# Layer 3's shared products of the first half behind the third quarter's experts, layer 0's later scans with their factor in PSUM, and layer 2's early adds left out

## The chip, the cores and the metric

The kernel runs on one core of one Trainium2 chip. The metric is device time in microseconds (us), the median over runs of the whole program; lower is better. All arithmetic is in float32 on the engines PE (matrix products), DVE (elementwise work on vectors), ACT (activation functions and copies) and POOL; SP only starts plain DMAs. POOL here does little but start indirect DMAs: each of its DMA_INDIRECT instructions scatters or gathers 128 rows of 128 numbers by a list of row positions.

## The reference: four layers over one stream of tokens

The input x has 4 batches of 1024 tokens of width 128. Each of the four layers adds a mixer, normalises, adds a feed-forward part, and normalises again:

```
x = layernorm(x + L0_attn(x)); x = layernorm(x + L0_ffn(x))
x = layernorm(x + L1_attn(x)); x = layernorm(x + L1_ffn(x))
x = layernorm(x + L2_attn(x)); x = layernorm(x + L2_ffn(x))
x = layernorm(x + L3_attn(x)); x = layernorm(x + L3_ffn(x))
```

- L0 mixer: running sums along the tokens. For each of 4 angles, a real and an imaginary part: `cumsum(p_w * poly * cos(phi))` and the same with the sine, both divided by `cumsum(p_w)`, then normalised, projected and gated. That is 8 running sums and one denominator over 1024 tokens.
- L0 feed-forward: one product of 128x128 with quantised operands.
- L1 mixer: a diagonal state-space recurrence. L1 feed-forward: 16 experts of which 4 are chosen for a token, and a shared network.
- L2 mixer: causal attention with 16 heads. L2 feed-forward: 8 experts, 2 chosen, on a common base.
- L3 mixer: products with Toeplitz matrices. L3 feed-forward, the one that the change reorders:

```
sel = expert_out at the 4 chosen of 32 experts;  out = sum(sel * topk_scores)
out = out + silu(flat @ sgate_w.T) * (flat @ sup_w.T) @ sdown_w.T     # shared, hidden width 512
```

## The kernel before: two orders laid over each other

**Tiles and parts.** The tokens are 32 tiles of 128 rows, held in SBUF as `self.x`. A quarter q is 8 tiles (two of each batch, 256 tokens along the sequence). Layer 0 and layer 3 work by quarters or halves: part a is quarters 0 and 1, b is quarter 2, c is quarter 3. Layer 1 has a and the rest r; layer 2 has parts a2, m2, n2.

**How experts are reached.** A router gives each token its experts and a position in a list in device memory. `spread` scatters the rows of a part into that list (one DMA_INDIRECT for each tile and choice, by `indirect`, L1327). The expert stage loads groups of 4 list tiles (`xg`, through SP's queue), multiplies them and writes its results to a second list. `collect` (L1437 and after) gathers for each token tile the rows of its chosen experts into a buffer `yt` and adds them to x on DVE (L1452). Its buffers come from a pool `yp` of 5 or 8.

**When collect adds.** An add is emitted when a landing is expected by the planner's clock `self.now`: while more than one tile is gathered, `self.spacing` is set (the caller wrapped the generator in `spaced`, which also makes each indirect DMA wait for the landing of the one two before it), and the oldest is due, the loop at L1466 adds at once. If all buffers are full it must add the oldest; what is left is added at the end. `spaced` collects occur in layer 1 (`l1_close`) and in layer 2 (`rows_in(a2)` beside `l2_attn(1)`, `rows_in(m2)` beside `l2_experts(n2)`).

**The order of the work.** All engines run their instructions in the order in which the program emits them. `mix(main, side, pace)` emits a main generator and, after each of its steps, lets a side generator advance by an amount given by the two generators' yields and the pace; `queued` fixes the emitted order on every engine. `press` advances the side until something is ready. So the pair (main, side) and the pace decide where on each engine's queue a side step stands.

**Layer 0's second half.** `l0_attn((2, 3))` runs as main with `spread("l1", a)` (64 scatters) beside it. Within it `prepare(q)` makes three products z in PSUM: the value xv (project(0)), the gate (project(1)) and the spread weight pwx; later rsx takes the same pool. Pool "l0z" holds two z buffers of [128 x 1024], two banks of PSUM each. `l0_scan` (L361 to L369) is the running sum: DVE's tensor_tensor_scan of out = keep * previous + source, where `keep` is a [128 x 1024] tile in SBUF, one except for zeros at the first token of each batch. For the denominator `den` the source is z in PSUM; for the real and imaginary parts (`s`) it is a tile in SBUF.

**The end.** In `all` (L2020 and after) the side generator `on` holds, in order: attention, routing and spread of b; then, side by side, `last(a)` (collect of a's 16 tiles, and `finish(a)`, the final normalisation and output, as soon as "shared l3a" is marked) and attention, routing and spread of c; then `last(b)`. The main sequence is experts(a), shared(a), shared(b), experts(b), shared(c), experts(c), close(c). `l3_shared` has 4 blocks of 512 tokens for a and 2 for b and c; a block is 4 rounds of products with `glu` (silu at L763, product `hs` at L764) and a product back (`py`). For a the result is added to x on DVE (L1768); for b and c it is kept in a tile `sh` by ACT (L1771), and `held` adds it when the experts begin. Experts stages end in an If that handles lists longer than expected; it holds work for all engines and is a border for the order of emission.

Of the kernel before, what the change touches and what calls it, by code (L numbers as in the profile page):

```python
# [15 lines left out]
ALU = mybir.AluOpType  # L16
AX = mybir.AxisListType
PSUM = bass.MemoryType.PSUM
DRAM = bass.MemoryType.DRAM

P = 128
# [10 lines left out]
QC = QT * P  # L32
# [3 lines left out]
KH, HC, MF, CK = 32, 4, 4, 4  # L36
# [38 lines left out]
class Kernel:  # L75
# [282 lines left out]
        for b in range(B):  # L358
            self.mm(ps[32 * b : 32 * b + 32, :], w, src[:, b * TQ : (b + 1) * TQ], start, stop)

    def l0_scan(self, out, src, i, q):  # L361

        nc = self.nc
        first = lambda a: a.rearrange("p (b t) -> p b t", b=B)[:, :, 0]
        if q:
            nc.vector.tensor_tensor(first(src), first(src), self.sums[:, i, :], ALU.add)
        nc.vector.tensor_tensor_scan(out, self.keep.rearrange("p b t -> p (b t)"), src, 0.0, ALU.mult, ALU.add)
        if q + 1 < NQT:
            nc.scalar.copy(self.sums[:, i, :], out.rearrange("p (b t) -> p b t", b=B)[:, :, TQ - 1])  # L369

# [7 lines left out]
    def l0_attn(self, qs):  # L378

        nc, tc, col = self.nc, self.tc, self.col
        ts, tt = nc.vector.tensor_scalar, nc.vector.tensor_tensor
        x, x0T, taps, cb = self.x, self.x0T, self.taps, self.col["conv_b"]
        with ExitStack() as ctx:
            bp, tp, psy = self.l0_bp, self.l0_tp, self.l0_psy
            psz = self.pool(ctx, "l0z", 2, space=PSUM)
            pss = self.side

            def prepare(q):  # L390
                z2 = self.tile(pss, [P, BLK], "s")[:, :TQ]
                for k in range(CK):
                    for b in range(B):
                        self.mm(
                            z2[32 * b : 32 * b + 32, :], taps[:, k, 2 * P :], x0T[:, q, b, k : k + TQ],
                            k == 0, k == CK - 1,
                        )
                pw = self.tile(bp, [P, TQ], "pw")
                ts(pw, z2, cb[:, 2:3], col["score"], ALU.add, ALU.mult)
                ts(pw, pw, -20.0, 20.0, ALU.max, ALU.min)  # L400
                nc.scalar.activation(pw, pw, AF.Exp)
                tt(pw, pw, self.tw[:, q, :], ALU.mult)

                def project(ch):
                    z = self.tile(psz, [P, QC], "z")
                    for h in range(2):
                        for k in range(CK):
                            self.mm(
                                z[:, h * BLK : (h + 1) * BLK].rearrange("p (b t) -> p b t", b=2),
                                taps[:, k, ch * P : (ch + 1) * P],  # L410
                                x0T[:, q, 2 * h : 2 * h + 2, k : k + TQ],
                                k == 0,
                                k == CK - 1,
                            )
                    return z

                z = project(0)
                xv = self.tile(bp, [P, QC], "xv")
                nc.scalar.activation(xv, z, AF.Identity, bias=cb[:, 0:1])
                z = project(1)  # L420
                gate = self.tile(bp, [P, QC], "gate")
                nc.scalar.activation(gate, z, AF.Silu, bias=cb[:, 1:2])
                pwx = self.l0_spread(psz, pw)

                pq = self.tile(bp, [P, QC], "pq")
                ts(pq, xv, self.nw2, self.dw[:, 1:2], ALU.mult, ALU.add)
                tt(pq, pq, xv, ALU.mult)
                nc.vector.scalar_tensor_tensor(pq, pq, self.dw[:, 0:1], pwx, ALU.add, ALU.mult)
                den = self.tile(bp, [P, QC], "den", bufs=1)
                self.l0_scan(den, pwx, 2 * MF, q)  # L430
                ts(den, den, 1e-4, None, ALU.max)
                nc.scalar.activation(den, den, AF.Square)
                return xv, gate, den, pq

            made = self.l0_made
            if not made:
                made[qs[0]] = prepare(qs[0])
                yield (20.0,)
            for q in qs:
                xv, gate, den, pq = made.pop(q)  # L440
                ms = self.tile(pss, [P, BLK], "s")[:, :TQ]
                self.l0_by_head(ms, self.headd, den, True, False)
                yv = self.tile(psy, [P, QC], "yv")
                for m in range(MF):

                    k = self.tile(tp, [P, QC], "k")
                    nc.scalar.activation(k, xv, AF.Identity, scale=self.turn[:, m : m + 1], bias=self.rnd)
                    nc.scalar.activation(k, k, AF.Identity, bias=self.drop)
                    nc.vector.scalar_tensor_tensor(k, xv, self.turn[:, m : m + 1], k, ALU.mult, ALU.subtract)
                    im = self.tile(tp, [P, QC], "im")  # L450
                    nc.scalar.activation(im, k, AF.Sin, scale=2.0 * PI_IN)
                    nc.scalar.activation(k, k, AF.Abs)
                    re = self.tile(tp, [P, QC], "re")
                    nc.scalar.activation(re, k, AF.Sin, scale=-2.0 * PI_IN, bias=self.halfpi)
                    for part, v in ((1, im), (0, re)):
                        tt(v, v, pq, ALU.mult)
                        s = self.tile(tp, [P, QC], "s", bufs=3)
                        self.l0_scan(s, v, 2 * m + part, q)
                        sq = self.tile(tp, [P, QC], "sq")
                        nc.scalar.activation(sq, s, AF.Square)  # L460
                        first, last = m == 0 and part == 1, m == MF - 1 and part == 0
                        for h in range(2):
                            c = slice(h * BLK, (h + 1) * BLK)
                            self.mm(yv[:, c], self.wbd[:, part * MF + m, :], s[:, c], first, last)
                        self.l0_by_head(ms, self.head, sq, False, last)
                        yield (5.0,)
                    if m == 0 and q + 1 in qs:
                        made[q + 1] = prepare(q + 1)
                        yield (10.0,)
                if q == 1:  # L470
                    self.l0_weight()
                    made[q + 1] = prepare(q + 1)
                rs = self.tile(bp, [P, TQ], "rs")
                nc.scalar.activation(rs, ms, AF.Sqrt, scale=1.0 / (2.0 * HC * MF))
                nc.vector.reciprocal(rs, rs)
                rsx = self.l0_spread(psz, rs)
                for g in range(2):
                    c = slice(g * BLK, (g + 1) * BLK)
                    tt(gate[:, c], rsx[:, c], gate[:, c], ALU.mult)
                    tt(gate[:, c], yv[:, c], gate[:, c], ALU.mult)  # L480
                for g in range(2):
                    po = self.tile(pss, [P, 4, D], "s")
                    for k in range(4):
                        t = g * 4 + k
                        self.mm(po[:, k, :], gate[:, t * P : (t + 1) * P], self.w_out)
                    t0 = q * QT + g * 4
                    tt(x[:, t0 : t0 + 4, :], po, x[:, t0 : t0 + 4, :], ALU.add)
                self.norm(self.quarter(q), by="act", on_act=True)
                yield (10.0,)
# [951 lines left out]
    def collect(self, lay, part, k, yp, first=0, nt=None, which=None):  # L1441

        nc = self.nc
# [3 lines left out]
        late = []  # L1447
# [9 lines left out]
        for t in which or range(first, first + (nt or part.nt)):  # L1457
            yt = self.tile(yp, [P, k, D], "yt")
            for i in range(k):
                self.indirect(  # L1460
                    out=yt[:, i, :], out_offset=None, in_=ys,
# [1 line left out]
                )  # L1463

            late.append((t, yt, self.moved_by + 4.0))
            while self.spacing and len(late) > 1 and late[0][2] <= self.now:  # L1466
                add()
            if len(late) == yp.bufs:
                while late[0][2] > self.now:
# [495 lines left out]
    def all(self):  # L1965
        a, rest = self.first, self.rest
        b, c = rest
        r = self.both[1]
        a2, m2, n2 = self.by_rows
        with ExitStack() as ctx:  # L1970
# [37 lines left out]
            with ExitStack() as c3:  # L2008
# [26 lines left out]
                    self.when(listed("made l3b")), self.last(b, yp),  # L2035
                )
                self.run(self.mix(self.l3_experts(a, wall3), on, 0.45, False))
                self.run(self.mix(self.chain(self.l3_shared(a, sw), self.mark("shared l3a")), on, 0.45, False))
                hold = self.pool(c3, "l3hold", 2)
                for p in (b, c):  # L2040
                    self.press(on, listed("mixed l3" + p.name))
# [3 lines left out]
                    self.press(on, listed("mixed l3c"))  # L2045
                    ahead = self.chain(self.held(p, sh), on) if p is c else self.held(p, sh)
                    self.run(self.mix(self.l3_experts(p, wall3, ahead), on, 0.75, False))
                self.run(self.close(c, yp))
        bad = self.nc.values_load(self.flag[0:1, 0:1], min_val=0, max_val=1)  # L2049
        with self.tc.If(bad > 0):  # L2050
# [181 lines left out]
```

## Time and profile before

| what | value |
|---|---|
| median of 9 runs | 2248.76 us (2236.59 to 2267.42) |
| the profiled execution's own time | 2228.34 us |
| its span | 2226.5 us |
| mean clock granted to PE | 0.849 |
| POOL's DMA_INDIRECT, layer 1's spread of a | 64, from 264.9 to 363.8 us |
| attention and routing of c done, spread of c | 32, from 1936.7 us |
| PE on shared(a), shared(b) | from 1863 to 2014 us |
| PE on experts(b), shared(c), experts(c) | 2017 to 2071, 2072 to 2094, 2097 to 2165 us |
| gathers of the last quarter (close) | 32, from 2170.6 to 2212.4 us |

The profiled execution is 0.9% faster than the median of the runs. A group line of the profile has the source line, the engine, the operation, out<-in by the program's names, and how often it ran, then busy time and the mean time of one in ns, then the idle time of the engine just before these instructions and what ended most of it. A line of the timeline has the start, the time taken, the engine, source line and operation; in brackets stands the idle time of the engine before it and what ended it. "issue" means that the engine waited for nothing that the profile shows; "remote" that what released it couldn't be named.

### The profile page before, as it was taken

The numbers are of one execution on the slowest core, as the hardware profiler recorded it, in microseconds if no ns is written. First come the engines' busy times: TensorE is split into PE (matmuls) and PEld (weight loads), VectorE is DVE, ScalarE is ACT, GpSimd is POOL, SyncE is SP. The second block draws the span as 40 slices with busy tenths as digits, with TensorE's granted clock in tenths as the row PEclk, the third lists the DMA queues.
The fourth block names the chain that finished last, engine by engine and source line by source line (L and its number), as shares of the span: only waits on it lengthen the run. The fifth ranks groups of instructions, "written<-read, shape, count | busy, mean of one in ns | idle before, by whom it ended". The sixth has DMA issues, their size and how long they took to land. (4 is left out here: it accounts for less than half of the span.)

```text
span 2226.5 us, 27104 instructions
## 1 busy us (share of the span) xinstructions
PE 1606.2 (72%) x9025; PEld 951.4 (43%) x9025; DVE 1196.7 (54%) x3491; ACT 903.8 (41%) x1352; POOL 681.6 (31%) x670
## 2 busy tenths in 40 slices
PE   7875864968486387789888788976987956718860
PEld 3332432844232146646522323322655734406650
DVE  8998783656665164436645555463423744503454
ACT  6873551423142263223257565653222631303340
POOL 1000284144406400534250000232463054362225
PEclk9986887988788698889999988997988978868985
DMA  9960012432401105323310000003422321013232
GB/s 296 287 185 1 8 47 91 119 117 98 146 30 50 42 16 195 117 68 88 116 41 8 1 1 1 20 21 146 186 81 82 93 79 53 22 47 105 86 115 58
DMA packets 215530, 187.10 MB, mean 84 GB/s; under 512 B 16528, under 2 KB 194064, under 8 KB 214864
## 3 DMA queue, kind: packets, MB, share of 16 engines
q1 hardware_dynamic: 194672, 142.29, 20.5%
q0 software_dynamic: 20704, 42.86, 5.9%
q8 instruction: 84, 1.38, 0.3%
q14 instruction: 70, 0.57, 0.1%
HBM read 88.49 MB, written 96.60 MB: 83 GB/s over the span
## 5 line engine op out<-in xcount | busy, mean ns | idle before, releaser
L1081 ACT ACTIVATE pr<-sc 128x1024 f32<-128x1024 f32 x288 | 279.7, 1021 | 255.5 <-PE sc L161 178.5
L161 PE MATMUL sc<-qm,kT 32*128 32x512 f32 (+3 forms) x1536 | 212.9, 575 | 44.1 <-ACT pr L1081 40.8
L161 PE MATMUL gu<-ld,xgT 128*128 x640 | 181.6, 431 | 68.3 <-ACT xgT L171 37.9
L161 PE MATMUL s<-pr,va 128*32 128x512 f32 (+3 forms) x1536 | 170.8, 541 | 39.4 <-DVE va L971 16.2
L1087 DVE TENSOR_TENSOR pr<-pr,ld 128x512 f32<-128x512 f32 (+1 forms) x160 | 91.7, 581 | 155.9 <-ACT pr L1081 134.2
L161 PEld LDWEIGHTS gu<-ld,xgT 128*128 128x128 f32 x640 | 129.5, 214 | 98.2 <-ACT xgT L171 49.3
L1814 DVE TENSOR_TENSOR hg<-sg,gu 128x256 f32<-128x256 f32 x160 | 66.3, 416 | 175.0 <-ACT sg L1813 108.7
L161 PEld LDWEIGHTS sc<-qm,kT 32*128 32x128 f32 x1536 | 87.5, 201 | 151.9 <-issue 70.4
L161 PE MATMUL gu<-wall,xgT 128*128 x304 | 148.0, 611 | 3.1 <-issue 1.7
L173 DVE COPY hT<-tp 128x512 f32<-128x512 f32 x118 | 81.0, 687 | 83.9 <-PE tp L169 63.6
L1813 ACT ACTIVATE sg<-gu 128x256 f32<-128x256 f32 x160 | 61.4, 385 | 146.1 <-PE gu L161 78.6
L169 PE MATMUL tp<-ld,hg 128*128 128x128 f32 x624 | 101.3, 283 | 10.8 <-DVE hT L173 7.5
L171 ACT COPY xgT<-tp 128x512 f32<-128x512 f32 x99 | 58.1, 587 | 125.2 <-PE tp L169 69.8
L169 PEld LDWEIGHTS tp<-ld,hg 128*128 128x128 f32 x624 | 80.6, 146 | 60.5 <-issue 36.9
L1569 ACT ACTIVATE sg<-gu 128x512 f32<-128x512 f32 x76 | 45.4, 597 | 145.8 <-PE gu L161 119.4
L161 PEld LDWEIGHTS s<-pr,va 128*32 128x32 f32 x1536 | 37.6, 114 | 145.5 <-issue 81.0
L161 PE MATMUL pu<-xT,ld 128*128 128x512 f32 x104 | 61.1, 678 | 51.8 <-DVE hs L764 51.2
L1327 POOL DMA_INDIRECT l1ra<-x,posl1a x64 | 79.7, 1245 | 60.3 <-DVE peq L1321 41.1
L764 DVE TENSOR_TENSOR hs<-sg,pu 128x512 f32<-128x512 f32 x48 | 32.6, 684 | 116.0 <-remote 70.2
L1327 POOL DMA_INDIRECT l1rr<-x,posl1r x64 | 63.6, 994 | 95.2 <-DVE posl1r L1302 71.3
L1327 POOL DMA_INDIRECT l2rm<-x,posl2m x16 | 15.9, 995 | 250.5 <-DVE peq L1320 243.2
L1571 DVE TENSOR_TENSOR hg<-sg,gu 128x512 f32<-128x512 f32 x76 | 51.9, 683 | 74.8 <-ACT sg L1569 64.1
(446 smaller groups left out, 3526.5 us busy)
## 6 DMA issues: line engine op xcount, KB each, us to landing
wall<-wall SPq DMA_DIRECT2D x16, 768.0 KB
l3ra<-zero SPq DMA_DIRECT2D x1, 6144.0 KB
ld<-in_l_w SPq DMA_DIRECT2D x2, 3072.0 KB
wall<-we SPq DMA_DIRECT2D x24, 256.0 KB
ld<-in_l_w SPq DMA_DIRECT2D x1, 6144.0 KB
l1ra<-zero SPq DMA_DIRECT2D x1, 5120.0 KB
l1rr<-zero SPq DMA_DIRECT2D x1, 5120.0 KB
xg<-l3ra SPq DMA_DIRECT2D x20, 256.0 KB
```

The costliest lines, as they stand in the source:

```text
L161: return self.nc.tensor.matmul(out, lhsT, rhs, start=start, stop=stop)
L169: nc.tensor.transpose(pt[:, k * P : (k + 1) * P], s, self.ident)
L171: nc.scalar.copy(dst, pt[:, : n * P])
L173: nc.vector.tensor_copy(dst, pt[:, : n * P])
L764: nc.vector.tensor_tensor(dst, sg, pu, ALU.mult)
L1081: nc.scalar.activation(pr, sc[h], AF.Exp)
L1087: nc.vector.tensor_tensor(d, d, cst["tril"].unsqueeze(1).unsqueeze(1).to_broadcast([P, 2, n, P]), ALU.mult)
L1327: ins = self.nc.gpsimd.indirect_dma_start(**kw)
L1569: nc.scalar.activation(sg, gu[:, 0, :], AF.Silu)
L1571: nc.vector.tensor_tensor(h, sg, gu[:, 1, :], ALU.mult)
L1813: nc.scalar.activation(sg, pg[:, :, 0, :], AF.Silu)
L1814: nc.vector.tensor_tensor(h[:, 2 * c : 2 * c + 2, :], sg, pg[:, :, 1, :], ALU.mult)
```

## The change

Three edits. First, in the second call of `l0_attn` the pool of z has one buffer instead of two, and the two banks hold `kept`, a copy of `keep` made by ACT; the scans of the real and imaginary parts of quarter 3, and the last three of quarter 2, take their factor from `kept`. The `den` scans and the others keep the SBUF tile. Second, the loop of early adds in `collect` runs for layer 1 only. Third, shared(a) is taken out from between experts(a) and shared(b) and put after experts(b), with pace 0.75 instead of 0.45, and the mark "shared l3a" goes with it.

```
-    def l0_scan(self, out, src, i, q):
+    def l0_scan(self, out, src, i, q, keep):
...
-        nc.vector.tensor_tensor_scan(out, self.keep.rearrange("p b t -> p (b t)"), src, 0.0, ALU.mult, ALU.add)
+        nc.vector.tensor_tensor_scan(out, keep, src, 0.0, ALU.mult, ALU.add)
...
-            psz = self.pool(ctx, "l0z", 2, space=PSUM)
+            psz = self.pool(ctx, "l0z", 1 if qs[0] else 2, space=PSUM)
             pss = self.side
+            held = self.keep.rearrange("p b t -> p (b t)")
+            if qs[0]:
+                keep = self.tile(self.pool(ctx, "l0k", 1, space=PSUM), [P, QC], "kept")
+                nc.scalar.copy(keep, self.keep.rearrange("p b t -> p (b t)"))
+            else:
+                keep = held
...
-                self.l0_scan(den, pwx, 2 * MF, q)
+                self.l0_scan(den, pwx, 2 * MF, q, held)
...
-                        self.l0_scan(s, v, 2 * m + part, q)
+                        self.l0_scan(s, v, 2 * m + part, q, keep if q > 2 or 2 * m + 1 - part > 4 else held)
...
-            while self.spacing and len(late) > 1 and late[0][2] <= self.now:
+            while self.spacing and lay == "l1" and len(late) > 1 and late[0][2] <= self.now:
                 add()
...
                 self.run(self.mix(self.l3_experts(a, wall3), on, 0.45, False))
-                self.run(self.mix(self.chain(self.l3_shared(a, sw), self.mark("shared l3a")), on, 0.45, False))
                 hold = self.pool(c3, "l3hold", 2)
                 for p in (b, c):
                     self.press(on, listed("mixed l3" + p.name))
                     sh = self.tile(hold, [P, QT, D], "sh")
                     self.run(self.mix(self.l3_shared(p, sw, sh), on, 0.75, False))
                     self.press(on, listed("l3" + p.name))
                     self.press(on, listed("mixed l3c"))
                     ahead = self.chain(self.held(p, sh), on) if p is c else self.held(p, sh)
                     self.run(self.mix(self.l3_experts(p, wall3, ahead), on, 0.75, False))
+                    if p is b:
+                        self.run(self.mix(self.chain(self.l3_shared(a, sw), self.mark("shared l3a")), on, 0.75, False))
                 self.run(self.close(c, yp))
```

## The prediction

> **What bounds the kernel now.** I read the engine totals first: no engine is busy all the way, so a stage has to be read by what it waits for.
>
> ```profile
> span 2226.5 us, 27104 instructions
> PE 1606.2 (72%) x9025; PEld 951.4 (43%) x9025; DVE 1196.7 (54%) x3491; ACT 903.8 (41%) x1352; POOL 681.6 (31%) x670
> L1327 POOL DMA_INDIRECT l1ra<-x,posl1a x64 | 79.7, 1245 | 60.3 <-DVE peq L1321 41.1
> ```
>
> The last line is the scatter of the first half's rows into layer 1's expert list: 64 instructions at a mean of 1245 ns, where other groups of the same kind have 978 to 995. The timeline at this group shows why, and what follows it.
>
> ```profile
> 279.55 2.28 DVE L367 TENSOR_TENSOR_SCAN den<-keep,z 128x1024 f32<-128x1024 f32 x1
> 280.77 0.96 POOL L1327 DMA_INDIRECT l1ra<-x,posl1a  x1 [0.30 <-issue]
> ...
> 285.20 2.23 DVE L367 TENSOR_TENSOR_SCAN s<-keep,im 128x1024 f32<-128x1024 f32 x1
> ...
> 285.42 2.78 POOL L1327 DMA_INDIRECT l1ra<-x,posl1a  x1 [0.31 <-issue]
> ...
> 294.43 2.94 POOL L1327 DMA_INDIRECT l1ra<-x,posl1a  x1 [0.30 <-issue]
> ...
> 362.80 0.96 POOL L1327 DMA_INDIRECT l1ra<-x,posl1a  x1 [0.30 <-issue]
> 368.88 0.69 DVE L848 TENSOR_TENSOR x<-py,x 128x512 f32<-128x512 f32 x1 [23.48 <-remote]
> 368.97 0.60 ACT L763 ACTIVATE sg<-pg 128x512 f32<-128x512 f32 x1 [15.37 <-remote]
> ```
>
> A DMA issue beside the `den` scan, whose source z is in PSUM, takes 0.96 us. Beside a scan with both operands in SBUF it takes 2.78 us and ends 0.77 us after the scan. And DVE and ACT, idle for 23.48 and 15.37 us, go on only 5 to 6 us after the scatter's last issue (362.80 + 0.96).
>
> Those waits are on PE's semaphore though PE's matmuls were long over. I looked for the same elsewhere: it happens only in long dense runs of indirect DMAs, most of all near the end. Busy time by window (PE, PEld, DVE, ACT, POOL, then clock, DMA share, GB/s), and the timelines of POOL, PE and DVE around it:
>
> ```profile
> 1900.00:1950.00 50.00, 45.88 (x192) 28.00 (x193) 30.84 (x111) 18.03 (x30) 13.05 (x14) 0.90 0.05 18
> 1950.00:2000.00 50.00, 6.20 (x32) 3.77 (x30) 1.07 (x5) 0.60 (x1) 36.21 (x38) 0.61 0.15 51
> ```
>
> ```profile
> 1936.68 0.99 POOL L1327 DMA_INDIRECT l3rc<-x,posl3c  x1 [33.29 <-ACT sg L763]
> ...
> 1996.54 0.94 POOL L1327 DMA_INDIRECT yt<-l3ya,posl3a  x1 [0.30 <-issue]
> ```
>
> ```profile
> 2004.45 2.07 PE L161 MATMUL pu<-xT,ld 128*128 128x512 f32 x2 [47.92 <-DVE hs L764]
> ```
>
> ```profile
> 2003.70 0.69 DVE L764 TENSOR_TENSOR hs<-sg,pu 128x512 f32<-128x512 f32 x1 [52.63 <-remote]
> ```
>
> While POOL issues 48 indirect DMAs back to back (32 of the spread of quarter c, 16 gathers of part a), PE idles 47.92 us, DVE 52.63. Last, layer 2's second attention call, DVE:
>
> ```profile
> 1122.08 0.35 DVE L1452 SCALAR_TENSOR_TENSOR x<-yt,wkl2a,x 128x128 f32<-128x128 f32 x1 [7.51 <-DMA yt<-l2ya,posl2a]
> 1123.61 0.35 DVE L1452 SCALAR_TENSOR_TENSOR x<-yt,wkl2a,x 128x128 f32<-128x128 f32 x1 [0.84 <-DMA yt<-l2ya,posl2a]
> ...
> 1129.23 0.35 DVE L1452 SCALAR_TENSOR_TENSOR x<-yt,wkl2a,x 128x128 f32<-128x128 f32 x1 [1.32 <-DMA yt<-l2ya,posl2a]
> ```
>
> DVE stands in front of gathered tiles that haven't landed; attention's L1087 multiply is queued behind, and PE waits 6.40 us for that (until 1130.30).
>
> **Part A: scan factor in PSUM.** The 11 scans changed (layer 0, quarter 2's last three and quarter 3's eight) are those whose starts lie between 265.2 and 317.7, inside the scatter (264.9 to 363.8). The 11 issues held by them take 15.8 us more than 0.96 each (1.01, 1.23, 2.57, 1.82, 0.87, 1.98, 1.86, 1.14, 0.91, 1.21, 1.22). With one SBUF operand they should run as beside `den`. Some of that returns: the issues then meet DVE's products with two SBUF operands (L456, 1.22 us; one beside it took 1.81). Stepping the queue at 1.26 us an issue along DVE's rows, the scatter ends 12.5 us sooner. The scan itself costs the same (`den` 2.28, s 2.23 to 2.29). Bounds of the gain: 0 to 15.8.
>
> The Trainium skill, "SBUF — State Buffer", section "Who interferes with whom", says that a VectorE instruction with two SBUF inputs contends with a GpSimd one that reads SBUF and that one with a single SBUF input does not, which agrees; its section "A bandwidth-pool intuition that's wrong (but worth ruling out)" lets the blocked side go on about 115 ns after VectorE's end, where the rows above show 0.77 us. By that figure the 11 issues would lose only about 8.6 us (15.8 less 11 x 0.65), an estimate from that page, and part A would be worth 6 rather than 12.5.
>
> Cost: z has one PSUM buffer, so project(1) (about 6.9 us of PE, 249.2 to 256.1) waits for the copy xv, 249.20 to 250.31: +1.1 us, and behind it on PE stands the router's mask product at 256.24, which leads to the scatter. The later uses have slack: the `den` scan has read z by 281.83, and rsx's matmul starts at 285.34. The copy into `kept` is one ACT pass of 128x1024, 1.04 us by the row of k at 278.43; ACT idles 3.05 us before 239.85, so nothing; uncovered it costs 1.04.
>
> What passes on: 12.5 - 1.1 = 11.4 if the 368.88 release follows the scatter's end. But a denser POOL may bring late PE semaphores into layer 0 itself, which has some 70 us left at 265. Before, with issues each 1.55 us on average, none is late before 339; the replayed pace is 1.32 until 282 and 1.48 until 316. Some lateness there I put at 2: **A = -9**. Bounds: -14.7 (15.8 - 1.1), and on the bad side the lock described as rival 1, +26.
>
> **Part B: layer 2's early adds.** The spaced collects of a2 (32 gathers, 1101.3 to 1159.8) and m2 now add only with all 8 buffers full, after 16 gathers, 25 us in, or at the end. The 12.5 us in which DVE stood on landings (7.51 + 0.84 + 0.86 + 1.26 + 0.76 + 1.32) go; on PE that is 6.40. Next late: the same adds, 16 at 0.35 = 5.6 us, in a bunch ahead of layer 3's attention of a, whose spread starts only at 1476. For m2 (8 tiles) the adds near 1661 to 1681 had no such waits: 0, within 3 either way. **B = -5**; bounds -12.5 and +5.6 (+3 more if m2's bunch shows).
>
> **Part C: shared(a) behind experts(b).** Nothing is added: 4 blocks of some 11 us of PE move. It moves past SP's loads of quarter b's 12 groups of list tiles, which now start earlier (b's scatter is done by 1838.5, so they wait for nothing), and past POOL's queue: first 32 gathers of a, spread c (32), the rest of a's gathers (32), then b's. Working the yields against both paces, c's spread starts in experts(b)'s sixth group, and of a's gathers only 4 follow it at once; the other 12 of the 16 come one tile at a time. The dense run shrinks from 48 to some 36 issues, 45.5 us instead of 60.9. PE's idle time began 19.9 us after the run's start and ended 6.9 after its end, so 47.9 becomes 32.5: -15.4. The run of 32 at 1797.7 to 1838.5 cost PE 24.74, which bounds the gain at 23; 0 if 12 gathers before it join up to 48 again, and below nothing, 10, if POOL's late gathers hold an expert group. The first 32 gathers (1863.4 to 1903.4, 20.75 us of PE idle) stay 32 in a row, now beside shared(b). I take half: **C = -8**. Cover: spread c must land before experts(c); it has about 80 us now and is later by some 50. finish(a) waits for the mark "shared l3a", which now comes after experts(b); by the yields it still falls into experts(c)'s groups 4 to 5, as before, and b's gathers into 6 to 12.
>
> **Sum.** -9 - 5 - 8 = -22 on the profiled execution's 2228.3 (span 2226.5, 1.8 around it), 2206. That execution lies 20.4 us, 0.9%, under the median 2248.8 of nine, so on the median's scale 2248.8 - 22 = **2227**.
>
> **Rivals.**
> 1. Layer 0 locks (slower). Scans no longer hold POOL back, so issues run at 1.26 us and late PE semaphores begin before 300, as in the other dense runs. Then layer 0's last 35 to 45 us run only after the scatter's end near 347, and the step now at 368.88 comes at about 392: +23 instead of -9. With B and C: 2248.8 + 23 - 13 = 2259, up to 2275 without them. For it: runs at 1.29 and 1.26 (1797.7, 1863.4) lock PE within 16 to 21 us. Against it: products and the 1.32 to 1.48 pace remain until 316. It decides from the point where PE's updates stay late for over 13 us before 320.
> 2. The tail (slower): a's finish slips past experts(c)'s sixth group, and b's 32 gathers (1.27 each, 41 us) come in front of the last quarter's 32. 2249 + 41 - 14 = 2276. Against: the computed place is unchanged.
> 3. Absorbed (no change): DVE has 48.5 of 50 us busy at 250 to 300 and sets layer 0's end itself; the dense run re-forms. A, B, C near 0, 2240 to 2255.
> 4. The change doesn't do what it says: a scan from PSUM still holds POOL since its output is in SBUF. A = +1, rest -13: 2237. The `den` row speaks against it.
>
> **Chances.** 2227 case 0.45 (own range 2208 to 2238), rival 1 0.22, rival 2 0.10, rival 3 0.15, rival 4 0.08. About 0.5% (11 us) is what a measurement can tell from nothing. Slower: 0.10 + most of 0.22 = 0.30. Same: rival 3 and part of 1 and 4, 0.17. Faster: the rest, 0.53. The range reaches to 2270: above it most of rival 2 and the extreme of rival 1, 0.12; below 2208, where all gains come near their bounds, 0.06.
>
> **What would show it.** A: issues beside the 11 scans at 0.96 us, scatter's group mean near 1050 ns, its end near 352, the x<-py release near 357 to 360. If its mean falls but the release is later than 369, rival 1. B: no DVE waits on yt near 1115 to 1130, PE's 6.40 gone. C: the longest PE idle near c's spread under 40 us. If it is still 48, or if gathers of l3yb stand among those of l3yc, C is wrong.

## The result: slower by 1.6%, and the profile after

The changed kernel takes 2281.56 us in the median of 20 runs (2254.04 to 2313.18), the kernel before 2248.53 in 62 (2217.11 to 2273.50). The ratio is 1.0159, with a 95% interval of 1.0131 to 1.0187. It was forecast as 2227 and lies outside the range up to 2270. The profiled execution took 2314.1, 1.4% more than its median, so stages are compared in it and not its total.

The group line of the scatter of the first half's rows and busy time by window in layer 0's last quarter (PE, PEld, DVE, ACT, POOL, clock, DMA share, GB/s), of the changed kernel, and below them the middle window of the kernel before:

```profile
L1333 POOL DMA_INDIRECT l1ra<-x,posl1a x64 | 62.7, 980 | 62.2 <-DVE peq L1326 43.0 <-issue 18.6 <-DMA l1ra<-x,posl1a 0.3
```

```profile
250.00:300.00 50.00, 25.76 (x137) 10.49 (x136) 33.56 (x119) 20.39 (x22) 26.23 (x26) 0.78 0.09 33
300.00:350.00 50.00, 1.08 (x8) 0.20 (x8) 0.00 (x0) 3.29 (x3) 36.50 (x38) 0.50 0.13 51
350.00:400.00 50.00, 31.30 (x142) 15.27 (x143) 39.09 (x53) 28.54 (x34) 0.00 (x0) 0.80 0.03 9
```

```profile
300.00:350.00 50.00, 36.45 (x149) 17.09 (x149) 28.41 (x59) 23.38 (x31) 39.49 (x35) 0.84 0.31 116
```

The mean issue fell from 1245 to 980 ns. Part of that is only that DVE does little beside it: from 300 to 350 DVE does nothing, and PE 1.08 us of work (36.45 before). Where DVE works on, the mean is 1068 (E10, below). The product of PE that makes z, DVE's timeline, with what it does on either side of the idle time, and POOL's last issue:

```profile
276.83 1.89 PE L161 MATMUL z<-pw,ld 128*128 128x256 f32 x8
```

```profile
293.17 1.28 DVE L434 SCALAR_TENSOR_TENSOR pq<-pq,dw,z 128x1024 f32<-128x1024 f32 x1 [14.09 <-remote]
...
299.08 0.68 DVE L437 TENSOR_SCALAR den<-den 128x1024 f32<-128x1024 f32 x1
355.20 1.75 DVE L481 RECIPROCAL rs<-rs 128x256 f32<-128x256 f32 x1 [55.44 <-ACT rs L480]
```

```profile
347.10 0.96 POOL L1333 DMA_INDIRECT l1ra<-x,posl1a  x1 [0.30 <-issue]
```

PE has ended z at 278.72. DVE needs it for the first instruction of its lines, but begins that only at 293.17, after 14.09 us of idle time. The profile can't name what released it ("remote"); that it is PE's semaphore is read from what the instruction takes in. The scatter ends 16 us earlier than before (348.1 against 363.8), and layer 0 stands still until 7 us after its end. Layer 1's first x<-py then comes at 407.5 instead of 368.9. The end of the changed kernel, PE's timeline (the three longest idle stretches from 1945 us on):

```profile
1981.29 2.07 PE L161 MATMUL pu<-xT,ld 128*128 128x512 f32 x2 [30.19 <-DVE hs L770]
...
2041.05 3.78 PE L161 MATMUL gu<-ld,xgT 128*128 x8 [17.41 <-issue]
...
2081.73 3.78 PE L161 MATMUL gu<-ld,xgT 128*128 x8 [34.43 <-DVE hT L173]
```

Before, the stretches at the same work were 20.75 and 47.92. Now they are 30.19, and 17.41 + 34.43.

### The profile page after: what moved, and what is told of

Its sections match the earlier page's. It is cut to its first block, busy times and chain, and to the rows that moved or that the text cites. A ratio compares the mean times of both kernels' runs of the same rounds, so it can differ in the third digit from the quotient of the medians.

```text
span 2312.2 us, 27088 instructions
## 1 busy us (share of the span) xinstructions
PE 1600.0 (69%) x9025; PEld 951.4 (41%) x9025; DVE 1197.4 (52%) x3491; ACT 900.9 (39%) x1351; POOL 662.0 (29%) x670
## 5 line engine op out<-in xcount | busy, mean ns | idle before, releaser
L173 DVE COPY hT<-tp 128x512 f32<-128x512 f32 x118 | 81.0, 687 | 87.5 <-PE tp L169 53.6
L1333 POOL DMA_INDIRECT l3ra<-x,posl3a x64 | 64.1, 1002 | 94.0 <-ACT pr L1087 64.2
L161 PE MATMUL yp<-ld,hT 128*128 x640 | 87.0, 278 | 3.5 <-DVE hT L173 3.4
L1333 POOL DMA_INDIRECT yt<-l3ya,posl3a x64 | 61.0, 954 | 97.8 <-DVE x L1458 55.7
L169 PE MATMUL tp<-ld,xg 128*128 128x128 f32 x396 | 69.0, 303 | 26.6 <-DMA xg<-l2rn 5.4
```

The source lines that it names most:

```text
L161: return self.nc.tensor.matmul(out, lhsT, rhs, start=start, stop=stop)
L169: nc.tensor.transpose(pt[:, k * P : (k + 1) * P], s, self.ident)
L173: nc.vector.tensor_copy(dst, pt[:, : n * P])
L1333: ins = self.nc.gpsimd.indirect_dma_start(**kw)
```

## The experiments

Each comparison below is with runs of the kernel before on the same chip, in the same session. The sessions fall into two kinds. In four the median of the kernel before was 2235 to 2273 us, as in the result; in three it was 1932 to 1933. I call the first kind sessions with late handoffs: there PE's semaphore reaches DVE and ACT several microseconds late within POOL's runs of indirect DMAs (it was read so in the prediction, and above for z), in the second kind it doesn't. The number of the chip doesn't tell them apart: chip 9 was met in both.

**Which edit costs: the three alone, and the first without its point.** The first edit alone (E1) has the one z buffer, `kept`, and the 11 scans from PSUM; E2 has only the condition `lay == "l1"`; E3 only moves shared(a). E4 is E1 with

```
-                        self.l0_scan(s, v, 2 * m + part, q, keep if q > 2 or 2 * m + 1 - part > 4 else held)
+                        self.l0_scan(s, v, 2 * m + part, q, held)
```

so that the z buffer and the copy stay and every scan reads its factor from SBUF.

> Before with the first edit alone (one z buffer, the kept copy, 11 scans with the factor in PSUM). Theory 'lock' (POOL's scatter, no longer held up by the scans, runs at 1.26 us an issue and PE's semaphore reaches DVE and ACT late for the rest of the run): the scatter ends near 348, DVE idles over 40 us before it, and the time is 30 to 38 us over before, nearly all that the whole change costs (33). Rival 'end' (most of the loss comes from the shared products moved behind experts(b)): within 12 us of before.

> Before with the second edit alone (early adds for layer 1 only). The profile of the changed kernel shows layer 2's second attention call about 8 us shorter between its gathers of a2 and the spread of m2, then 10 us lost by the spread of n2. Theory: the waits on landings go, the time is 0 to 8 us under before. Rival: the bunched adds come back later and it is 0 to 5 us over before.

> Before with the third edit alone (shared(a) behind experts(b)). Theory 'same density': POOL has the same number of back-to-back indirect DMAs, only beside other work, and PE's idle time moves (47.9 in one piece becomes two pieces of about 17 and 34, the 20.8 before it about 30): 0 to 13 us over before. Rival, as predicted: 8 us under before. Rival 'end': 25 to 33 us over.

> The first edit with its one z buffer and its copy into PSUM, but with every scan's factor read from SBUF as in before. Theory 'lock': the scans hold POOL up again, so the time is that of before plus 0 to 2 us (the single z buffer), the scatter ends near 364. Rival 'z buffer' (what costs is the second product waiting for the first one's copy): 30 us or more over before, as with the whole edit.

Measured, in one session with late handoffs: E1 1.0130 (1.0063 to 1.0197), E2 1.0017 (0.9985 to 1.0048), E3 1.0028 (0.9986 to 1.0069), E4 1.0026 (0.9967 to 1.0085). The three edits add up to 1.75%, the whole change has 1.59%. So the first edit carries the loss, and in it the scans' factor: E4 keeps all the rest and is back at before. The intervals of E1 and E4 overlap by a little, but their traces stand clearly apart: the first x<-py of layer 1 comes at 394.83 in E1 and at 367.20 in E4. "End" and "z buffer" fall. The window 300 to 350 of E1 and then of E4:

```profile
300.00:350.00 50.00, 6.71 (x25) 4.61 (x26) 14.49 (x15) 13.32 (x14) 38.41 (x39) 0.53 0.13 51
```

```profile
300.00:350.00 50.00, 33.89 (x136) 15.40 (x136) 28.92 (x60) 23.83 (x30) 39.34 (x36) 0.82 0.31 116
```

POOL issues hardly more in this window (39 against 36), but over the whole scatter at a mean of 1.33 us instead of 1.52. DVE's idle time between the scatter's first and last issue is 50.7 us in E1, 33.7 in E4, 36.3 in before, 63.5 in the whole change. E1's 394.83 is 26 us after before's 368.88.

In E2 DVE's waits for gathered tiles of a2 fall from 12.6 us to 4.5 (their group by tile, of E2), and the time doesn't move clear of noise:

```profile
L1452 DVE SCALAR_TENSOR_TENSOR x<-yt,wkl2a,x x32: 335/347/365, 1125.3 to 1181.1; 128x128 f32<-128x128 f32 x32
...
  DMA yt<-l2ya,posl2a: 4.5, 4
```

The stage from these gathers to the scatter of m2 is 6.6 us shorter in E2's trace than in before's, but from that scatter to the next one of a it takes 11.8 us more. POOL, on its side, waits 13.8 us for gather buffers where it waited 5.4. What takes the gain back was not followed.

In E3, POOL's timeline at c's scatter shows why the long run did not shrink:

```profile
1936.95 0.95 POOL L1327 DMA_INDIRECT yt<-l3ya,posl3a  x1 [37.02 <-DVE x L1452]
...
1951.10 0.95 POOL L1327 DMA_INDIRECT yt<-l3ya,posl3a  x1 [0.30 <-issue]
1952.36 0.99 POOL L1327 DMA_INDIRECT l3rc<-x,posl3c  x1 [0.30 <-issue]
...
1992.30 0.96 POOL L1327 DMA_INDIRECT l3rc<-x,posl3c  x1 [0.30 <-issue]
1993.57 0.98 POOL L1327 DMA_INDIRECT yt<-l3ya,posl3a  x1 [0.30 <-issue]
```

Twelve gathers before the 32 scatters and four behind are again 48 in a row; PE's idle time there is 22.91 + 29.12 instead of 47.92, and 30.13 instead of 20.75 in the first run.

**Breaking the run by waits.** In `all`, layer 1's scatter of a is wrapped so that every fourth issue waits for the landing of the one before it: E5 on top of the first edit, E6 on before. E7 does it on before to layer 3's scatters of b and c and the gathers of a, E8 to all of these and to the scatter of r (where before already had a wait at every issue, for the landing two before it).

```
-                    self.run(self.mix(self.l0_attn((2, 3)), self.spread("l1", a, K1)))
+                    self.run(self.mix(self.l0_attn((2, 3)), self.spaced(self.spread("l1", a, K1), 4, 1, 1.6)))
```

> The first edit, with layer 1's scatter of part a made to pause: every fourth indirect DMA waits for the landing of the one before it. Theory 'lock by density' (what costs is the unbroken run of issues 1.26 us apart, not the factor in PSUM nor anything else of the edit): with the pauses PE's semaphore arrives in time again, DVE's idle time before the scatter's end goes from about 50 us to under 15, and the time is back at before, within 8 us. Rival 'a queue that is longer by count' (64 DMAs of software descriptors in flight hold PE's semaphore, however spaced): still 25 us or more over before.

> Before, its scans untouched, with the same pauses in that scatter. Theory 'lock by density': the pauses also break the dense second half (from 321 us on), so the 19 to 23 us in which PE, ACT and DVE wait for 368.9 shrink, if the scatter doesn't end later than about 372: 0 to 12 us under before. Rival: the scatter only ends later, 5 to 15 us over before.

> Before, with the same pauses in layer 3's dense runs: the spreads of b and c and the gathers of a (runs of 32, 32 and 48 at 1.26 to 1.29 us an issue, with 24.7, 20.8 and 47.9 us of PE idle). Theory 'lock by density': the three idle stretches fall together by 40 us or more and the time by 20 to 50. Rival 'longer by count': the idle stretches grow with the runs' length, 5 to 30 us over before.

> Before, with the pauses in layer 1's scatters of a and of r and in layer 3's runs. Theory: the gains of the single places add up, and the 37 us of PE idle in the scatter of r (719 to 761) shrink as well: 30 to 70 us under before. Rival: 10 us or more over before.

These met a session without late handoffs: before took 1933.17. E5 0.9960 (0.9944 to 0.9975), E6 1.0017 (1.0003 to 1.0031), E7 1.0082 (1.0065 to 1.0099), E8 1.0107 (1.0090 to 1.0124). So nothing was decided on the lock; what they show is that where layer 3 has no long idle stretches to win back, the pauses cost some 16 us (E7). In E7's trace 56 gathers of b and c stand in one row at the end (1864.8 to 1939.6), most of b's behind experts(c), which PE ends at 1872.5.

**The change itself in such a session.** The same kernels again, with the whole change (E9), the first edit alone (E10), E5's and E7's kernels (E11, E12).

> The whole changed kernel again. The last four runs met a chip on which the kernel before takes 1933 and no handoff of PE is late in any run of indirect DMAs; the ones before it a chip where it takes 2235 and they are. Theory 'lock of the chip' (the loss exists only where PE's semaphore is held up): on a chip of the first sort the changed kernel is 5 to 20 us under before, on one of the second 25 to 40 over. Rival 'order' (the loss is in the order of the work itself): over before by 25 or more on both.

> The first edit alone again. Theory 'lock of the chip': where before takes about 1933, the scatter ends near 348 and layer 1 goes on at once, 7 to 13 us under before; where it takes about 2235, 25 to 35 over. Rival 'order': 25 or more over before on both.

> The first edit with the pauses in the scatter, again. Where before takes 1933 it was 8 us under before. Where before takes 2235: theory 'lock by density': the pauses lift the lock and it is within 10 us of before; rival 'longer by count': 25 us or more over.

> Before with pauses in layer 3's runs, again. Where before takes 1933 there was no PE idle time to win, and it was 16 us over, because a's gathers took POOL longer and b's came after experts(c). Where before takes 2235: theory 'lock by density': the idle stretches of 24.7, 20.8 and 47.9 us shrink by 40 or more together and the time falls by 10 to 40; rival: 10 to 30 us over before.

Before took 1931.69. E9 0.9963 (0.9950 to 0.9977), E10 0.9973 (0.9960 to 0.9985), E11 0.9973 (0.9962 to 0.9984), E12 1.0102 (1.0088 to 1.0117). The same instructions are 0.4% faster than before here and 1.6% slower there: the rival "order" falls, since it asked for the loss in both. The window of E10, to be held beside E1's, which is the same kernel, and its handoff of z:

```profile
300.00:350.00 50.00, 45.39 (x211) 23.67 (x210) 36.76 (x80) 27.69 (x42) 38.78 (x37) 0.91 0.32 120
```

```profile
276.09 1.89 PE L161 MATMUL z<-pw,ld 128*128 128x256 f32 x8
```

```profile
278.30 1.27 DVE L434 SCALAR_TENSOR_TENSOR pq<-pq,dw,z 128x1024 f32<-128x1024 f32 x1
```

POOL issues nearly as densely (1.37 us in the mean over the scatter, 1.33 in E1; its first ten issues 1.29 here and 1.31 there and in the changed kernel), and PE works 45.39 us instead of 6.71. DVE takes z 0.32 us after PE's end, in the changed kernel's profile 14.45 us after it. To the scatter the first edit does what the prediction said: the 64 issues take from 266.3 to 353.8, 87.5 us, against 98.8 for the same scatter of unchanged code in E7, 11.3 sooner where 12.5 were replayed. But the release does not follow the scatter's end here: the first x<-py comes at 339.07, and at 338.70 in E7. What comes sooner are the first results of layer 1's experts, at 380.7 instead of 388.9. Of this 5.2 us are left in the time, where 7 to 13 were expected.

**Waits again.** E13 to E15 are E5's, E7's and E6's kernels, sent to meet the other kind of session.

> The first edit with pauses in the scatter. On a chip with late handoffs (before about 2235): theory 'lock by density' within 10 us of before, DVE idle before the scatter's end under 15 us; rival 'the factor in PSUM' 25 us or more over before, as without pauses. On a chip without: 5 to 8 us under before, as twice already.

> Before with pauses in layer 3's runs. With late handoffs: theory 'lock by density' 10 to 40 us under before; rival 10 to 30 over. Without: 16 to 20 us over, as twice already.

> Before with pauses in layer 1's scatter of a. With late handoffs: theory 0 to 12 us under before. Without: 2 to 4 us over, as once already.

They met one without late handoffs once more (before 1931.77) and repeat: 0.9962 (0.9947 to 0.9976), 1.0092 (1.0063 to 1.0121), 1.0012 (0.9996 to 1.0029).

> The first edit with pauses in the scatter, once more. With late handoffs (before about 2235): theory 'lock by density' within 10 us of before, DVE idle before the scatter's end under 15 us; rival 'the factor in PSUM' 25 us or more over before. Without: 5 to 9 us under before, as three times already.

E16, E5's kernel, met late handoffs (before 2237.62): 1.0116 (1.0037 to 1.0195). By the expectation as written the rival "factor in PSUM" wins. But POOL's timeline shows that the waits did not hold it:

```profile
302.92 0.96 POOL L1333 DMA_INDIRECT l1ra<-x,posl1a  x1 [0.30 <-issue]
304.18 0.96 POOL L1333 DMA_INDIRECT l1ra<-x,posl1a  x1 [0.30 <-issue]
305.44 0.96 POOL L1333 DMA_INDIRECT l1ra<-x,posl1a  x1 [0.30 <-issue]
306.71 0.96 POOL L1333 DMA_INDIRECT l1ra<-x,posl1a  x1 [0.30 <-issue]
```

The issues are still 1.26 us apart; the mean over the scatter is 1.34, as in E1, and DVE is idle for 51.3 us of it, as in E1. Of POOL's idle time in the scatter only 0.3 us ended with a landing. The run was another E1, on another chip, and did not test density. E5 and E11 are no test of pauses either: there the waits moved the mean pace from E10's 1.37 us to 1.40.

**Breaking the run by work.** E17 has the first edit and puts six memsets of a 128x128 tile on POOL after every fifth indirect DMA, ordered behind it and ahead of the next, in layer 1's scatters, layer 3's scatters of b and c and the gathers of a. E18 adds the scatters of a2, m2 and of layer 3's a, and the gathers of b.

```
+    def breathe(self, on):
+        self.rests += on
+        if on and self.rests % 5 == 0:
+            for _ in range(6):
+                m = self.nc.gpsimd.memset(self.pad, 0.0)
...
+                self.moved.append(m.ins.name)
...
+                self.breathe(lay + part.name in ("l1a", "l1r", "l3b", "l3c"))
...
+                self.breathe(lay + part.name == "l3a")
```

> The first edit, and after every fifth indirect DMA of layer 1's scatters (a and r), layer 3's scatters (b and c) and the gathers of a, six memsets of 128x128 on POOL (about 0.23 us each by before's row, so some 1.4 us of rest in 7.7). Waits on landings had not thinned the scatter, this must. With late handoffs (before about 2235): theory 'density' DVE is idle less than 25 us within the scatter of a (the first edit alone: about 50 before its end), layer 1 goes on at most 10 us later than in before, and the idle stretches of r, b, c and a shrink by a third or more; time 0 to 60 us under before. Rival 'the factor in PSUM' or 'count': DVE idle as in the first edit alone, 25 to 60 us over before. Without late handoffs (before about 1932): 5 to 20 us over before, for POOL's longer chains.

> The run before with rests also in the scatters of a2, m2 and of layer 3's a, and in the gathers of b. With late handoffs (before 2235 to 2275): theory 'density': PE's idle stretch near b's gathers (24.5 us) goes below 12 and the time is 6 to 9% under before; rival: it stays, 5 to 6.5% under. Without late handoffs (before about 1932): 5 to 20 us over before, POOL's chains being some 12% longer with nothing to win.

Both met late handoffs. E17: 0.9339 (0.9259 to 0.9419), 2122.49 against 2273.30. E18: 0.8985 (0.8932 to 0.9038), 2031.43 against 2268.26. POOL's timeline and the window of E17:

```profile
304.97 1.36 POOL L1335 DMA_INDIRECT l1ra<-x,posl1a  x1 [0.30 <-issue]
306.64 0.96 POOL L1335 DMA_INDIRECT l1ra<-x,posl1a  x1 [0.30 <-issue]
307.59 1.54 POOL L1385 MEMSET pad<- 128x128 f32 x6
309.29 0.96 POOL L1335 DMA_INDIRECT l1ra<-x,posl1a  x1 [0.16 <-issue]
```

```profile
300.00:350.00 50.00, 44.87 (x203) 23.52 (x204) 37.66 (x81) 27.45 (x41) 39.07 (x69) 0.90 0.30 111
```

The factor is in PSUM as in E1, the 64 scatters are all there, and PE has 44.87 us of work in the window instead of 6.71. What differs are the memsets and the pace that they make, 1.62 us in the mean. So the factor in PSUM is not what holds PE, and neither is the count: it is the unbroken run of issues. Two quite different things break it, POOL's stalls behind the scans (E4) and these memsets (E17); a pause of a third kind was not tried. The scatter ends at 370.4, 18 us later than in E1, and the first x<-py is at 342.1 instead of 394.8, where sessions without late handoffs have it at 338 to 342. (DVE's idle time within the scatter is 32.9, over the 25 that were expected: some 20 of it lie at the end, where DVE waits for a product of POOL's, `qt`, that stands behind the scatter in POOL's queue.) The gain is far over the 0 to 60 us that were expected of E17, and a little over the 6 to 9% of E18. At layer 3's end, where PE did 6.20 us of work in 50 before, it does 41.23 (E18, from c's scatter at 1814.6):

```profile
1815.00:1865.00 50.00, 41.23 (x240) 34.56 (x238) 18.03 (x45) 16.90 (x38) 38.98 (x74) 0.93 0.42 132
```

PE's idle stretches of over 8 us, without the one at the program's start, add up to 193.8 us in before's trace, 307.9 in the changed kernel's, 248.7 in E1, 80.8 in E17 and 67.7 in E18, and in the session without late handoffs to 48.6 in E9 and 38.1 in E10; the one of 24.5 us near b's gathers in E17 is gone in E18. E18 beats the kernel before by 10% in a session with late handoffs (the changed kernel wasn't run there). That is 237 of the 336 us that lie between the 2268 us of the kernel before there and its 1932 us without late handoffs; what the other 100 are was not followed. E18 was not tried in a session without late handoffs, nor was a kernel with these rests and without the first edit, so how much of the 10% the first edit gives or takes is open.

## Why the prediction was wrong

**Part A, the failed step.** The prediction costed late semaphores within layer 0 at 2 us ("Some lateness there I put at 2"), because none was late there before 339 at a mean pace of 1.55, and the replayed pace of 1.32 to 1.48 seemed slow enough until 316. It was not slow enough. In the changed kernel z is late 13 us after the scatter's start (ended by PE at 278.72, taken by DVE at 293.17), and up to there POOL issued 1.31 us apart: the replayed pace of 1.32 came true, what was concluded from it did not. The 1.55 is also a mean over the whole scatter; in its first 26 us the kernel before issues 1.91 us apart. The prediction had named the sign itself, a lower mean issue with a release later than 369, and both came (980 ns, 407.5). That was rival 1, given 0.22: it put the release at 392 and the time at 2259, up to 2275 without B and C. E1 measured 394.8 for the release and +29 us (1.3%), where the rival had +23 for the edit. The choice between the ends failed, not the ends: -14.7 to +26 were on the page, and E1 lies 3 us over the upper one. It was taken from the row of the irregular run, 1.55, where the rows of the dense ones, 1.26 to 1.29, were nearer to the replayed start, 1.32, and these showed PE locked within 16 to 21 us.

The mechanism that the gain was worked from holds for the scatter. In E10 ten issues take over 1.1 us: the very first, and nine that end 0.83 us after a product of DVE with two SBUF operands; none ends so after a scan from `kept`. The scatter is 11.3 us shorter (87.5 in E10, 98.8 in E7); the 82.0 of the change and the 84.7 of E1 count DVE's standstill too. That the release follows the scatter's end holds only where handoffs are late. The Trainium skill, "SBUF — State Buffer", section "Who interferes with whom", agrees in kind: a scan with one SBUF operand no longer delays the DMA issue. The estimate of 6 us made with that page's figure of about 115 ns (section "A bandwidth-pool intuition that's wrong (but worth ruling out)") set two different things against each other: 115 ns is when the blocked side goes on, and 0.77 us, in the rows, is when the issue has ended. So these rows don't contradict the page, and the 6 us don't follow from it; the measured 11.3 us in E10 stands by the 12.5 worked out from the trace. The +1.1 for the single z buffer was of the right size: the scatter starts at 266.1 instead of 264.9 (E4, with the one buffer as well, 265.7; E1 267.3). One reading was loose without bearing on the sum: the other scatters have group means of 959 to 1001 ns and the gathers 946 to 1040, not 978 to 995.

**Part B**: forecast -5, measured +4, with an interval of -3 to +11. Most of the waits went (12.6 to 4.5, and with them PE's 6.40), the stage got shorter by about the size predicted (6.6), and the gain was gone one stage later. It was counted at the place of the wait without asking what the next stage waits for.

**Part C**: forecast -8, measured +6 (-3 to +15). The step that failed is the count of 36: the prediction had "0 if 12 gathers before it join up to 48 again" as a bound, and they did, in E3 and in the whole change. The first 32 gathers did stay 32 in a row, but beside shared(b) they cost PE 9 us more (30.13 for 20.75), which the sum had at nothing.

**What wasn't on the list.** That the release at 368.88 is no need of the work was read rightly (it comes at 338.70 in E7, with the same layer 0), but the prediction took the lateness as a property of the kernel. It isn't: the same code, nearly as densely issued, shows none of it in three sessions, and there the whole change gains 7 us (E9) where 22 were forecast.

## What to carry to other kernels

When an edit removes a stall of one queue, ask what that stall was spacing out: here the scans that held POOL back were what let PE's semaphores through. Where the trace has rows of the same resource at the pace that the edit leads to, cost it by these and not by the row before. And a cure is only tested if its trace shows that it took effect: the waits on landings moved the pace by some 0.03 us, six small memsets at every fifth issue gave 7 to 10% of the time.

## What the runs showed of the hardware

- Long runs of indirect DMAs, 1.26 to 1.34 us apart, hold PE's semaphore back from DVE and ACT in some sessions (ACT idle for up to 40.74 us and DVE for 55.44 in one piece), and not in others with the same code; the kernel before takes 2235 to 2273 us in the first and 1932 to 1933 in the second. What sets the kind of session is not known.
- 1.5 us of memsets on POOL after every fifth issue lift it in the scatter of layer 1 (first x<-py at 342.1 in E17 and 340.9 in E18, for 394.8 in E1). Over the whole kernel they won back 237 of 336 us in E18.
- Waits on earlier landings hardly thin this scatter: in E16 0.3 us of POOL's idle time ended with a landing, and the mean pace was 1.34 us, for 1.33 in E1.
- A DMA issue beside a scan with its factor in PSUM is not held (0.96 us in E10); beside a scan or product of DVE with both operands in SBUF it takes up to 3.53 us and ends 0.77 to 0.83 us after that (before and E10).
